# Empty places of a token list: a real token with weight zero, or a token number past the end

## The chip, the cores and the metric

The kernel runs on one core of one Trainium2 chip. The metric is the device time of one execution in microseconds (us); lower is better. In the profile PE is the matrix engine (PEld its weight loads), DVE the vector engine, ACT the scalar engine, POOL the general engine that also issues the indirect DMAs, and SP the engine that issues most plain DMAs.

## The reference

A block with two halves. The first is a gated recurrent layer over 4 sequences of 1024 tokens of width 256. The second is a mixture of experts: each token is given to the two best of eight experts, and the two results are weighted and added to the token. All arithmetic is float32.

```python
h = _layernorm(x) * (1 + ca) + sa
x = x + ga * attn(h)              # rms norm, four 256x512 products, sigmoid gates,
                                  # a scan over the tokens, a 512x256 product, + h
h = _layernorm(x) * (1 + cb) + sb
gate = softmax(h @ Wg + bg); topk_scores, topk_idx = top_k(gate, 2)
combine_w = normalised topk_scores, put at topk_idx
for e in range(8):
    y = _gelu(h @ W1[e] + b1[e]) @ W2[e] + b2[e]
    output = output + y * combine_w[..., e:e + 1]
x = x + gb * output
```

## The kernel before

**First half.** The 4096 tokens go through in eight chunks of 512 (`c_` from 0 to 7, two for each sequence `b`). The order of work on every engine is written out by hand. In a chunk, `project(c_, hc)` is called for four column groups (`hc` 0 to 3), and each issues four products on PE (L432). Between them stand the steps of neighbouring chunks: for the next chunk `a_square`, `a_root` (L387), `a_scale` (L391 to L394) and `a_turn` (transposes on PE, L406); for the chunk before it `o_pe` (L469), `o_resid`, `f_stats` (L216) and `f_norm`; for the one before that `f_turn` and `f_gate`. The square roots of `a_root` and of the two norms are done on POOL as a power (`L387`, `L216`), so the chain for the next chunk's transposes is: ACT squares, DVE L386, POOL L387, DVE L391 to L394, PE L406.

**Routing.** Once a sequence `b` is complete, `r_first`, `r_second`, `r_rank_pe` and `r_place` work out, for each token and each of its two experts, its place in that expert's list. The lists are one DRAM tensor `lists`: a region of 4096 places for each expert and one spare block of 256, and a place holds a pair (token number, weight). `pre`, built at the start by a memset, an iota and a bitwise_and (L188, L189, L266), fills all places first with (place mod 256, weight 0). `r_place` puts the writes of the real pairs into a waiting line, 16 scatters of 128 pairs for a sequence (8 columns for each of the two choices, "in"). For sequence 0 it puts 32 further scatters ahead of them (4 columns by 8 experts, "out"; L673 to L701): they write pairs of weight 0 into the first 256 places of an expert, counted back from the end, with tokens that did not choose this expert, so that a block whose list turns out short doesn't name one token twice. `drain(n)` takes `n` scatters off the line and issues each on POOL behind a tiny memset of `between` (L564, L568). It is called with 6 after each `project`. The first "in" scatter waits for all "out" scatters to have landed. A scatter's semaphore is one of eight used in turn, so from the ninth on each one waits for the landing of the eighth before it.

**Second half.** The lists are cut into blocks of 256 places, `j` from 0. The first 8 blocks use tokens of sequences 0 and 1 alone and start in the last chunk. For each block `fetch_rows` gathers its 256 rows of `hx` (normed token and gate, 2 KB each) into `hb` by two indirect DMAs of 128 rows (L836), `fetch_entries` loads the pairs into `ent` (L823), `fetch_weights` loads 2 MB of weights (L854, L856), `b_turn` transposes (L878), `b_up` and `b_down` multiply (L894, L912), and two indirect DMAs add the results into the rows of `out` (L926). `fetch(j)` issues the gathers of block `j + 2` and the weights of `j + 1`. A block that has at most 128 real places is computed as a half block (`_True` in the profile; its second half is gathered but not multiplied); from block 32 on each block stands inside a branch that asks whether it exists. An `ent` buffer is used again four blocks later, an `hb` buffer three blocks later.

Of the kernel before, what the change touches and what calls it, by code (L numbers as in the profile page):

```python
# [9 lines left out]
F32 = mybir.dt.float32  # L10
I32 = mybir.dt.int32
AF = mybir.ActivationFunctionType
ALU = mybir.AluOpType
# [6 lines left out]
def tile_adaln_block(  # L20
# [32 lines left out]
    nc = tc.nc  # L53
    P = 128
    B, S, D = x.shape
    H = W_out.shape[0]
    E, _, F = W1.shape
    T = B * S
# [8 lines left out]
    TK = 256  # L67
    HK = TK // P
    LN_EPS = 1e-5
    RMS_EPS = 1e-8  # L70
    TOPK_EPS = 1e-8
    FAR = float(1 << 20)
    NJ = (2 * T + E * (TK - 1)) // TK
    BPE = T // TK
    NE = 8
# [7 lines left out]
    lists = dram.tile([n_places, 2], I32, tag="lists", name="lists")  # L83
# [8 lines left out]
    small = ctx.enter_context(tc.tile_pool(name="small", bufs=2))  # L92
    xpool = ctx.enter_context(tc.tile_pool(name="blocks", bufs=2))
# [91 lines left out]

    n_pre = n_places // P
    pre = setup.tile([P, n_pre, 2], I32, tag="pre", name="pre")
    nc.gpsimd.memset(pre, 0)  # L188
    nc.gpsimd.iota(pre[:, :, 0], [[1, n_pre]], base=0, channel_multiplier=n_pre % TK)  # L189

    expo = const.tile([P, 2, TPB], F32, tag="expo", name="expo")
    nc.gpsimd.memset(expo[:, 0, :], -0.5)
# [70 lines left out]
    nc.scalar.dma_start(out=b1_sb, in_=b1.rearrange("e (c p) -> (e c) p", p=P))  # L263
    nc.scalar.dma_start(out=wg_sb, in_=Wg.rearrange("(k p) e -> p k e", p=P))
    nc.scalar.dma_start(out=bg_sb, in_=bg.rearrange("(o e) -> o e", o=1).broadcast_to((P, E)))
    nc.vector.tensor_single_scalar(pre[:, :, 0], pre[:, :, 0], TK - 1, ALU.bitwise_and)  # L266
    X[0]["stats"] = stats(X[0]["x"], "a0")
    shift(0)
    a_norm(0)
# [50 lines left out]
    def load_mda(b: int):  # L320
        if b < B:
            MDA[b] = deep.tile([P, 2, D], F32, tag="mda", name=f"mda_{b}")
            nc.sync.dma_start(out=MDA[b], in_=rows[b : b + 1, :2, :].broadcast_to((P, 2, D)))
# [209 lines left out]
    R = {}  # L533
# [17 lines left out]
            R[b]["p"][:, ts(i, TPB), :], pl, bg_sb.unsqueeze(1).broadcast_to((P, TPB, E))  # L551
        )

    scattered = {"out": [], "in": []}

    waiting = []
    between = const.tile([P, 1], F32, tag="between", name="between")

    def scatter(place, what, kind):
        waiting.append((place, what, kind))  # L560

    def drain(n: int):
        for _ in range(min(n, len(waiting))):
            nc.gpsimd.memset(between, 0.0)  # L564
            scatter_now(*waiting.pop(0))

    def scatter_now(place, what, kind):
        ins = nc.gpsimd.indirect_dma_start(  # L568
            out=lists[:, :],
            out_offset=IndirectOffsetOnAxis(ap=place, axis=0),  # L570
            in_=what,
            in_offset=None,
            bounds_check=E * T - 1,
            oob_is_err=False,
        )

        for other in scattered[kind]:
            tc.declare_no_dep(ins.ins, other.ins, reason="other places")
        if kind == "in" and not scattered[kind]:
            wait_for(ins, scattered["out"])  # L580
        scattered[kind].append(ins)

    def r_softmax(b):
        p = R[b]["p"]
# [82 lines left out]
    def r_place(b):  # L667
        pick, pay, key, pr = (R[b][n] for n in ("pick", "pay", "key", "pr"))
        rank = small.tile(sh, F32, tag="rank", name=f"rank_{b}", bufs=1)
        nc.vector.tensor_add(rank, pr[:, :NT, :], over(count))  # L670
        nc.vector.tensor_add(count, count, pr[:, NT, :])

        if b == 0:  # L673

            nm = 2 * HK
            shn = [P, nm, E]
            gap = small.tile(shn, F32, tag="gap", name="gap", bufs=1)
            at = small.tile(shn, F32, tag="at", name="at", bufs=1)  # L680
            no = small.tile(shn, F32, tag="no", name="no", bufs=1)
            ati = small.tile(shn, I32, tag="ati", name="ati", bufs=1)
            payn = small.tile([P, nm, 2], I32, tag="payn", name="payn", bufs=1)
            nc.gpsimd.memset(payn, 0)
            nc.vector.tensor_copy(payn[:, :, 0], token[:, :nm])

            nc.vector.tensor_sub(
                gap, token[:, :nm].unsqueeze(2).broadcast_to(tuple(shn)), rank[:, :nm, :]
            )
            nc.vector.scalar_tensor_tensor(  # L690
                at, gap, -1.0, head.unsqueeze(1).broadcast_to(tuple(shn)), ALU.mult, ALU.add
            )
            nc.vector.tensor_scalar(no, gap, float(TK), FAR, ALU.is_ge, ALU.mult)
            nc.vector.tensor_add(at, at, no)
            nc.vector.scalar_tensor_tensor(
                at, R[b]["chose"][:, :nm, :], FAR, at, ALU.mult, ALU.add
            )
            nc.vector.tensor_scalar_add(ati, at, float(TK - 1))
            for n in range(nm):
                for e in range(E):  # L700
                    scatter(ati[:, n, e : e + 1], payn[:, n, :], "out")  # L701

        nc.vector.tensor_add(rank, rank, over(head))
        for r in range(2):
            place = small.tile([P, NT], F32, tag=f"place{r}", name=f"place{r}_{b}")
            placei = small.tile([P, NT], I32, tag=f"placei{r}", name=f"placei{r}_{b}")
            nc.vector.tensor_mul(key, pick[r], rank)
            nc.vector.tensor_reduce(place, key, AX.X, ALU.add)
            nc.vector.tensor_copy(placei, place)
            for n in range(NT):  # L710
                scatter(placei[:, n : n + 1], pay[r][:, n, :], "in")


    def blocks_of(shift: float):
# [84 lines left out]
    def turns(pool, n: int, shape, dtype, tag: str, j: int):  # L799

        slots = kept.setdefault(tag, [None] * n)
        if slots[j % n] is None:
            slots[j % n] = pool.tile(shape, dtype, tag=f"{tag}{j % n}", name=f"{tag}_{j % n}", bufs=1)
        return slots[j % n]

    def seen(j: int):
        return EARLY_B * S if j < NE else T
# [57 lines left out]
    def wait_for(ins, others):  # L865
        for other in others:
            tc.add_manual_dep(
                ins.ins, other.ins.name,
                mybir.DependencyInfo(mybir.DependencyClass.Sync, mybir.DependencyReason.DATA),
                reason="all of it is there",  # L870
            )
# [35 lines left out]
    def b_down(j: int, half: bool = False, mid=None):  # L907
        g, w2, b2b, ent, hb = (BK[j][n] for n in ("g", "w2", "b2b", "ent", "hb"))
        for t in range(1 if half else HK):
            py = ps_y.tile([P, D], F32, tag="y", name=f"pye_{j}_{t}_{half}")  # L910
            for fc in range(FC):
                nc.tensor.matmul(  # L912
                    py,
                    lhsT=g[:, fc, ts(t, P)],
                    rhs=w2[:, fc, :],
                    start=(fc == 0),
                    stop=(fc == FC - 1),
                )
            yb = xpool.tile([P, D], F32, tag="yb", name=f"yb_{j}_{t}_{half}", bufs=4)
            nc.vector.tensor_add(yb, py, b2b)  # L920
            nc.vector.scalar_tensor_tensor(  # L921
                yb, yb, ent[:, t, 1:2].bitcast(F32), hb[t][:, D:], ALU.mult, ALU.mult
            )
            if t > 0:
                nc.gpsimd.memset(between, 0.0)
            ins = nc.gpsimd.indirect_dma_start(  # L926
                out=out_rows[: seen(j)],
                out_offset=IndirectOffsetOnAxis(ap=ent[:, t, 0:1], axis=0),
                in_=yb, in_offset=None, bounds_check=seen(j) - 1, oob_is_err=True,
                compute_op=ALU.add,  # L930
            )
            for other in BK[j]["acc"]:
                tc.declare_no_dep(ins.ins, other.ins, reason="a block's tokens are distinct")
            BK[j]["acc"].append(ins)
            if t == 0 and mid is not None:
                mid()
# [20 lines left out]
    for c_ in range(NCH):  # L957
# [40 lines left out]
        if not more:  # L998
            fetch_weights(0)
            for j in range(NE):  # L1000
                fetch_entries(j)

            wait_for(BK[0]["ld"], scattered["out"] + scattered["in"])
            fetch_rows(0)
            fetch_rows(1)
        if part == 0:
            if c_ == 0:
                setup_ctx.close()
                pools["w"] = ctx.enter_context(tc.tile_pool(name="weights", bufs=2))
            load_gb(b)  # L1010
            load_mda(b + 1)
            if c_ == 0:
                load_mdf(1)

# [85 lines left out]
    for j in range(3, sure_whole):  # L1100
        fetch(j)
        drain(5)
        if j + 2 == NE:
            wait_for(BK[NE]["ld"], scattered["in"])
            for ins in BK[NE]["gathers"]:
                wait_for(ins, hx_stores + hx_gates)
        work(j)
        if j == NE:
            for ins in BK[j]["acc"]:
                wait_for(ins, x1_stores)  # L1110
# [52 lines left out]
```

## Time and profile before

| | |
|---|---|
| time, median of 3 runs | 830.62 us (830.11 to 831.63) |
| the profiled execution's own time | 836.73 us |
| its span, first to last instruction | 835.0 us |
| PE busy | 806.2 us, 97% |
| POOL busy | 332.9 us, 40% |
| POOL, 32 "out" scatters (L568 `lists<-payn,ati`) | 32.8 us, mean 1024 ns |
| POOL, 64 "in" scatters (L568 `lists<-pay,placei`) | 66.0 us, mean 1031 ns |
| POOL, gathers of `hb` from `ent` (L836) | 60, mean 1058 ns |
| POOL, additions into `out` of whole blocks, `ent` (L926) | 46, mean 1602 ns |
| granted PE clock, mean | 0.988 |
| bytes moved by DMA | 136.53 MB |

An engine's busy time is a sum over instructions. A "wait" line names who ended an engine's idle time. The profiled execution took 6.1 us longer than the median of the unprofiled ones.

### The profile page before, as it was taken

Reading aid. Unit: us, or ns where it says so; the run is one execution under the profiler, and the core shown is the slowest. Engines: PE = TensorE matmul, PEld = TensorE weight load, DVE = VectorE, ACT = ScalarE, POOL = GpSimd, SP = SyncE. Lnnn points to the kernel's source line nnn. Section 1 sums busy time; section 2 is a strip of 40 time slices with the busy share of each in tenths; the row PEclk is TensorE's granted clock in tenths of the full one; section 3 lists DMA queues with packets and bytes.
Section 4 is the critical chain, followed back from the end, with each engine's and each line's share of the span. In section 5 each row is a group of like instructions: output and inputs, shape, how many; then the busy total and the mean of one; then the engine's idle time right before and its main releaser. Section 6 shows DMA issues by size and latency. Waiting matters only on the chain. (4 is left out here: it accounts for less than half of the span.)

```text
span 835.0 us, 10666 instructions
## 1 busy us (share of the span) xinstructions
PE 806.2 (97%) x3447; PEld 607.7 (73%) x3447; DVE 349.9 (42%) x814; ACT 250.9 (30%) x577; POOL 332.9 (40%) x438
## 2 busy tenths in 40 slices
PE   6999999999979999999999999999999999999983
PEld 2454656465636467888888888888888888888973
DVE  4787776798569757444111111111121212111211
ACT  4434343534343425131313122222222121312221
POOL 2001010116577843478844343424343333434432
PEclk9999999999989999999999999999999999999997
DMA  8041221118301356397878787777777777878795
GB/s 304 0 130 44 90 89 62 51 44 75 46 27 32 77 134 208 91 257 194 207 230 228 205 211 219 210 200 222 204 208 219 208 228 203 230 201 224 210 335 182
DMA packets 111217, 136.53 MB, mean 164 GB/s; under 512 B 25576, under 2 KB 94252, under 8 KB 111152
## 3 DMA queue, kind: packets, MB, share of 16 engines
q1 hardware_dynamic: 86624, 102.15, 42.1%
q0 software_dynamic: 18800, 28.81, 15.2%
q10 hardware_dynamic: 5728, 4.77, 2.5%
q8 instruction: 33, 0.54, 0.3%
q14 instruction: 32, 0.26, 0.1%
HBM read 113.92 MB, written 21.78 MB: 163 GB/s over the span
## 5 line engine op out<-in xcount | busy, mean ns | idle before, releaser
L912 PE MATMUL pye_False<-w,g_False 128*128 128x256 f32 x992 | 220.9, 381 | 1.1 <-DVE x L482 1.1
L894 PE MATMUL ph_False<-xT,w 128*128 128x256 f32 x992 | 219.2, 379 | 0.0
L894 PEld LDWEIGHTS ph_False<-xT,w 128*128 128x128 f32 x992 | 188.3, 190 | 25.5
L912 PEld LDWEIGHTS pye_False<-w,g_False 128*128 128x128 f32 x992 | 187.1, 191 | 25.6 <-issue 1.1
L903 ACT ACTIVATE g_False<-ph_False,bb 128x256 f32<-128x256 f32 x248 | 104.1, 471 | 313.1 <-issue 225.6
L926 POOL DMA_INDIRECT out_dram<-yb_False,ent x46 | 73.7, 1602 | 188.5 <-DVE yb_False L921 188.5
L880 DVE COPY xT<-ptx 128x512 f32<-128x512 f32 x37 | 25.5, 690 | 200.5 <-PE ptx L878 200.5
L920 DVE TENSOR_TENSOR yb_False<-pye_False,b2b 128x256 f32<-128x256 f32 x62 | 26.3, 424 | 155.0 <-PE pye_False L912 155.0
L836 POOL DMA_INDIRECT hb<-hx,ent x60 | 63.5, 1058 | 28.0 <-issue 16.1
L568 POOL DMA_INDIRECT lists<-pay,placei x64 | 66.0, 1031 | 15.7 <-issue 11.8
L432 PE MATMUL pu<-hT,wu_sb 128*128 128x512 f32 x128 | 61.9, 607 | 0.0
L432 PE MATMUL pk<-hT,wk_sb 128*128 128x512 f32 x128 | 61.0, 599 | 1.0 <-ACT hT L408 1.0
L432 PE MATMUL pgo<-hT,wu_sb 128*128 128x512 f32 x128 | 60.6, 596 | 0.0
L432 PE MATMUL pgi<-hT,wu_sb 128*128 128x512 f32 x128 | 60.1, 592 | 0.0
L469 PE MATMUL pya<-wo,z 128*128 128x256 f32 x256 | 56.6, 379 | 0.0
L469 PEld LDWEIGHTS pya<-wo,z 128*128 128x128 f32 x256 | 48.6, 190 | 9.5 <-issue 3.3
L216 POOL TENSOR_TENSOR rstd_f<-rstd_f,expo 128x4 f32<-128x4 f32 x8 | 8.2, 1026 | 101.3 <-DVE rstd_f L215 101.3
L432 PEld LDWEIGHTS pgo<-hT,wu_sb 128*128 128x128 f32 x128 | 24.7, 193 | 31.5 <-issue 27.6
L432 PEld LDWEIGHTS pgi<-hT,wu_sb 128*128 128x128 f32 x128 | 24.3, 190 | 30.6 <-issue 30.6
L432 PEld LDWEIGHTS pu<-hT,wu_sb 128*128 128x128 f32 x128 | 24.2, 195 | 27.4 <-issue 25.2
L432 PEld LDWEIGHTS pk<-hT,wk_sb 128*128 128x128 f32 x128 | 23.1, 190 | 25.1 <-issue 20.7
L568 POOL DMA_INDIRECT lists<-payn,ati x32 | 32.8, 1024 | 20.6 <-DMA lists<-payn,ati 13.1
(198 smaller groups left out, 781.1 us busy)
## 6 DMA issues: line engine op xcount, KB each, us to landing
w<-in_L_ffn_W_dram SPq DMA_DIRECT2D x74, 1024.0 KB, 6.5
b2b<-in_L_ffn_b_dram SPq DMA_DIRECT2D x37, 128.0 KB, 6.8
hx<-gb ACTq DMA_DIRECT2D x4, 1024.0 KB, 8.8
out_dram<-x SPq DMA_DIRECT2D x8, 512.0 KB, 4.0
hx<-h SPq DMA_DIRECT2D x8, 512.0 KB, 4.1
x<-in_L_attn_x_dram SPq DMA_DIRECT2D x7, 512.0 KB, 6.7
wu_sb<-in_L_attn_W_ugg_dram SPq DMA_DIRECT2D x3, 512.0 KB, 6.9
mdf<-rows SPq DMA_DIRECT2D x4, 384.0 KB, 8.1
```

Source lines behind the costliest of these rows:

```text
L216: nc.gpsimd.tensor_tensor(rstd, rstd, expo[:, 0, :], ALU.pow)
L432: nc.tensor.matmul(ps, lhsT=w[:, k, col : col + P], rhs=hT[:, k, :], start=(k == 0), stop=(k == KC - 1),)
L469: nc.tensor.matmul(py[:, t, :], lhsT=z[hc][:, ts(2 * q + t, P)], rhs=wo[:, hc, :], start=(hc == 0), stop=(hc == HC - 1),)
L568: ins = nc.gpsimd.indirect_dma_start(out=lists[:, :], out_offset=IndirectOffsetOnAxis(ap=place, axis=0), in_=what, in_offset=None, bounds_ ...
L836: nc.gpsimd.indirect_dma_start(out=g, out_offset=None, in_=hx[: seen(j), :], in_offset=IndirectOffsetOnAxis(ap=BK[j]["ent"][:, t, 0:1], ax ...
L880: nc.vector.tensor_copy(xT, pt)
L894: nc.tensor.matmul(ph[:, u, :], lhsT=w1[:, k, ts(fc, P)], rhs=xT[:, k, :n], start=(k == 0), stop=(k == KC - 1),)
L903: nc.scalar.activation(g[:, fc, :n], ph[:, u, :], AF.Gelu_apprx_tanh, bias=bb[:, fc : fc + 1])
L912: nc.tensor.matmul(py, lhsT=g[:, fc, ts(t, P)], rhs=w2[:, fc, :], start=(fc == 0), stop=(fc == FC - 1),)
L920: nc.vector.tensor_add(yb, py, b2b)
L926: ins = nc.gpsimd.indirect_dma_start(out=out_rows[: seen(j)], out_offset=IndirectOffsetOnAxis(ap=ent[:, t, 0:1], axis=0), in_=yb, in_offse ...
```

## The change

The list is filled with token number T (4096, one past the last) instead of place mod 256, so the iota and the bitwise_and go. The gathers leave such rows out and keep what the buffer held; the additions leave them out too (`oob_is_err` becomes False). In the early blocks the bound is 2048. As the rows left in `hb` must be numbers, all six `hb` buffers are cleared once, on POOL in chunk 1 ahead of that chunk's `a_root`. The 32 "out" scatters, their places and their wait are gone. In the text of the loop, `load_mdf(1)` of chunk 0 ends up below a condition that never holds, so that load is gone; the same rows are loaded again in chunk 1 as before.

```diff
-    nc.gpsimd.memset(pre, 0)
-    nc.gpsimd.iota(pre[:, :, 0], [[1, n_pre]], base=0, channel_multiplier=n_pre % TK)
+    nc.gpsimd.memset(pre, T)
...
-    nc.vector.tensor_single_scalar(pre[:, :, 0], pre[:, :, 0], TK - 1, ALU.bitwise_and)
...
-        if kind == "in" and not scattered[kind]:
-            wait_for(ins, scattered["out"])
...
-        if b == 0:
...
-            nc.gpsimd.memset(payn, 0)
...
-            for n in range(nm):
-                for e in range(E):
-                    scatter(ati[:, n, e : e + 1], payn[:, n, :], "out")
...
             for n in range(NT):
-                scatter(placei[:, n : n + 1], pay[r][:, n, :], "in")
+                waiting.append((placei[:, n : n + 1], pay[r][:, n, :]))
...
+    def clear_rows():
+
+        for j in range(3):
+            for t in range(HK):
+                nc.gpsimd.memset(turns(xpool, 3, [P, 2 * D], F32, f"hb{t}", j), 0.0)
...
-                in_=yb, in_offset=None, bounds_check=seen(j) - 1, oob_is_err=True,
+                in_=yb, in_offset=None, bounds_check=seen(j) - 1, oob_is_err=False,
                 compute_op=ALU.add,
...
         if part == 0:
             if c_ == 0:
...
             load_gb(b)
             load_mda(b + 1)
+        elif c_ == 1:
+            clear_rows()
             if c_ == 0:
                 load_mdf(1)
```

More of the change, by code (lines that the diff above doesn't have):

```diff
@@ L71, in tile_adaln_block @@
     TOPK_EPS = 1e-8
-    FAR = float(1 << 20)
     NJ = (2 * T + E * (TK - 1)) // TK
@@ L552, in f_gate @@
         )
-    scattered = {"out": [], "in": []}
+    scattered = []
     waiting = []
     between = const.tile([P, 1], F32, tag="between", name="between")
-    def scatter(place, what, kind):
-        waiting.append((place, what, kind))
     def drain(n: int):
@@ L564, in drain @@
             nc.gpsimd.memset(between, 0.0)
[L565 to L578, printed above, removed]
-        if kind == "in" and not scattered[kind]:
-            wait_for(ins, scattered["out"])
-        scattered[kind].append(ins)
+            place, what = waiting.pop(0)
+            ins = nc.gpsimd.indirect_dma_start(
+                out=lists[:, :],
+                out_offset=IndirectOffsetOnAxis(ap=place, axis=0),
+                in_=what,
+                in_offset=None,
+                bounds_check=E * T - 1,
+                oob_is_err=False,
+            )
+            for other in scattered:
+                tc.declare_no_dep(ins.ins, other.ins, reason="other places")
+            scattered.append(ins)
     def r_softmax(b):
@@ L671, in r_place @@
         nc.vector.tensor_add(count, count, pr[:, NT, :])
-        if b == 0:
[L677 to L683, printed above, removed]
-            nc.gpsimd.memset(payn, 0)
[L685 to L698, printed above, removed]
-            for n in range(nm):
-                for e in range(E):
-                    scatter(ati[:, n, e : e + 1], payn[:, n, :], "out")
         nc.vector.tensor_add(rank, rank, over(head))
@@ L1001, in tile_adaln_block @@
                 fetch_entries(j)
-            wait_for(BK[0]["ld"], scattered["out"] + scattered["in"])
+            wait_for(BK[0]["ld"], scattered)
             fetch_rows(0)
@@ L1103, in tile_adaln_block @@
         if j + 2 == NE:
-            wait_for(BK[NE]["ld"], scattered["in"])
+            wait_for(BK[NE]["ld"], scattered)
             for ins in BK[NE]["gathers"]:
```

## The prediction

> **What bounds the kernel now.** I read the page's busy times first, then the slices, then who waited, then the order of time around the one hole. (The chain that ended last has three pieces and tells nothing here.)
>
> ```profile
> PE 806.2 (97%) x3447; PEld 607.7 (73%) x3447; DVE 349.9 (42%) x814; ACT 250.9 (30%) x577; POOL 332.9 (40%) x438
> PE   6999999999979999999999999999999999999983
> POOL 2001010116577843478844343424343333434432
> PEclk9999999999989999999999999999999999999997
> ```
>
> PE is the bound nearly everywhere: only slices 1, 12 and the last two (20.9 us each) have holes. Freeing POOL or the DMAs is worth something only there. Slice 12 is also where POOL is fullest and the clock dips. PE's own waits name the cause:
>
> ```profile
> PE pta L406 <- DVE u L394: 4.6, 1, 4.6
> ```
>
> In order of time on PE (start, duration, then the idle time before it):
>
> ```profile
> 195.41 1.04 PE L406 MATMUL pta<-ident,u 128*128 128x128 f32 x8
> ...
> 238.05 2.05 PE L406 MATMUL pta<-ident,u 128*128 128x128 f32 x8 [4.56 <-DVE u L394]
> 239.89 3.62 PE L432 MATMUL pu<-hT,wu_sb 128*128 128x512 f32 x4
> 243.31 2.35 PE L432 MATMUL pgo<-hT,wu_sb 128*128 128x512 f32 x4
> 245.50 1.88 PE L432 MATMUL pk<-hT,wk_sb 128*128 128x512 f32 x4
> ```
>
> The transposes of chunk 6 come 4.56 us late, and the next products run at half speed: from the transposes to the next pk takes 7.45 us here (238.05 to 245.50) and 4.31 us a chunk earlier (195.41 to 199.72). The hole costs 4.56 + 3.14 = **7.7 us**. Who is late is on POOL:
>
> ```profile
> 211.46 1.60 POOL L568 DMA_INDIRECT lists<-payn,ati  x1 [7.58 <-DMA lists<-payn,ati]
> ...
> 222.50 0.97 POOL L568 DMA_INDIRECT lists<-payn,ati  x1 [5.50 <-DMA lists<-payn,ati]
> ...
> 227.32 1.06 POOL L216 TENSOR_TENSOR rstd_f<-rstd_f,expo 128x4 f32<-128x4 f32 x1
> ...
> 236.02 1.07 POOL L387 TENSOR_TENSOR ss<-ss,expo 128x4 f32<-128x4 f32 x1
> ```
>
> The power for a_root (L387) had its operand at 223.50 (DVE L386, 223.34 + 0.16), but stood behind 24 "out" scatters, two of which waited 7.58 and 5.50 us for earlier ones to land. It ran 12.5 us late; DVE L391 to L394 and PE follow.
>
> The other hole is the end. Half blocks follow each other every 7.46 us while nothing is late (787.02 to 794.48); the next three steps take 9.78, 9.45 and 8.70 us, 5.5 us too much. Block 35 (j from 0) is the last.
>
> ```profile
> 795.19 0.37 SPq L823 DMA_DIRECT2D ent<-lists  x1
> ...
> 801.60 1.05 POOL L836 DMA_INDIRECT hb<-hx,ent  x1 [4.09 <-PE pye_True L912]
> ...
> 809.62 0.55 PE L878 MATMUL ptx<-ident,hb 128*128 128x128 f32 x3 [1.17 <-DMA hb<-hx,ent]
> ```
>
> The add of block 31 (issued 788.51) lands, by the DMA view 5.3 to 7.4 us later, and only then does SP load the pairs of block 35 into the same buffer (795.19); those rows are gathered from 801.60 on, and PE waits for them at 809.62. The end thus hangs on landings: add, pairs, gather, and at last the final add (823.67).
>
> **What the Trainium skill says.** TensorE: Matmul & The Clock Gate, "Part 1: The HAM clock gate (the "warmup" mystery)": after an idle window of about 3.4 us the clock falls to half, and about 3.4 us of work bring it back. The trace agrees: after 4.56 us of idling the granted clock is 0.50 from 238 to 244 us. DMA: Bandwidth & Descriptors, "SWDGE vs HWDGE vs iDMA": for DMAs issued from GpSimd, indirect ones included, software there computes the descriptors. The trace shows about 1 us of POOL for each, and the same for scatters whose entries are nearly all left out (974 ns median of the 32 "out") as for full ones (979). I know of no price there for an entry that a bound leaves out.
>
> **The change part by part**, against the profiled execution's 836.73 us.
>
> 1. *32 "out" scatters gone.* 32.8 us busy, 33 memsets and 20.6 us of idling leave POOL. The 16 "in" scatters take their slots: 6 and 6 in chunk 4, 4 in chunk 5, instead of 24 ahead of L387. Suppose the same waits at the same places: the 14th is done at 216.9, the 15th waits to 222.50, the 16th ends at about 224.8. L216 then runs to 225.9 and L387 to 226.9, against 237.09. The transposes could start 10.2 us earlier, at 227.9; PE frees itself at 233.49. So the hole closes with 5.6 us to spare: **-7.7 us**. In chunk 6 L387 (276.45) stood behind scatters too, without a hole on PE (279.77); it now stands ahead of them.
> 2. *The wait of the first "in" scatter* (3.02 us at 251.69) goes; POOL only, no PE hole there: 0. POOL at 277 to 299 also loses its backlog, so the last pairs for the early blocks land sooner, and PE did not wait for block 0's rows at 317.68: 0. Everything there moves with PE; SP still has w and b2b ahead of the pairs (302.09 against 304.04), so at most 2 us of earliness is to be had, nothing that PE waits for.
> 3. *Seven small DVE operations of r_place* (187.12 to 188.36, and 0.84 us of waiting) go; DVE had u of chunk 5 ready at 191.4 and PE transposed it at 195.41: 0.
> 4. *Six memsets of hb* in chunk 1. Nearest row: L188, 128x516 int32, 0.53 us, so 3.2 us. They follow L216 (ends 67.89) and end near 71.1; L387 comes at 73.02. Cover: DVE's project work. Without it (memsets at twice the price) L387 is 1.3 us late, and u is ready at 76.9 for transposes at 81.01: 0.
> 5. *Front:* the iota (0.36 us) and bitwise_and (0.29) go. PE's first product also needs sc, ready at 4.01 (DVE); bn_stats may start 0.2 us sooner if x has landed. The first projections begin at 20.34 behind that chain: 0 to -0.2, taken -0.1.
> 6. *load_mdf(1) of chunk 0:* one SP issue of 0.42 us (46.61) and 384 KB; the x load behind it lands long before its use: 0.
> 7. *Entries left out.* 36 blocks are computed (31 whole, 5 half), 38 gathered: 9728 rows for 8192 real pairs, so 1536 rows of 2 KB, 3.1 MB of 136.5, are not moved, and 384 of 8576 additions. Whole blocks hide it (PE without idle from 366 to 788). At the end each half block loses at least 256 KB (its second half) of some 2.8 MB (2 MB weights, 128 KB b2b, 512 KB rows, 128 KB additions), while the DMAs are 81% busy: 9% of the load. That entries left out move no bytes is seen on two quiet stretches with seven scatters each, nearly all out of range in the first and all real in the second:
>
> ```profile
> q0 software_dynamic: 224, 0.00, 1.5%
> ...
> q0 software_dynamic: 224, 0.01, 1.8%
> ```
>
>    Against it, they land no sooner: 7.6, 8.6, 7.5 and 5.3 us for out-of-range scatters from 237 to 243, where full ones took 4.6, 5.1, 5.9 and 6.3 from 251 to 258, a mean of 7.25 against 5.5. Bounds: the lost 5.5 us and about 1 us of the final landing come back (-6.5), or the three hops through leave-outs (add, gather, final add) are 1.8 us later each (+5.4). I take -0.7: less load and slow landing nearly cancel, in favour of less load because 252 GB/s are flowing there.
> 8. *Additions with leave-out.* Not shown before. Upward bound 0.6 us more for each, downward the 1031 ns of a leave-out scatter, 0.57 less. Two of them lie on the end's path: -1.1 to +1.2, taken 0. Elsewhere POOL is at 38%.
>
> Sum in the profiled execution: -7.7 - 0.1 - 0.7 = -8.5, to 828.2. It is 6.1 us above the median of the runs. PE's stream cannot be quicker without a profile, so those 6.1 lie in waits: front 6.0, this hole 7.7, one at 340 us 2.6, tail 5.5, after the last PE work 12.6, outside the span 1.7, in all 36.1. Spread evenly, the hole is 7.7 x (1 - 6.1/36.1) = 6.4 us in the runs. I take 6.4 + 0.1 + 0.7 = 7.2: 830.6 - 7.2 = **823.4 us**.
>
> **The rivals.**
> - *The hole is mostly the profile's.* If the landings that POOL waited for are quicker unprofiled (13.1 us of waits in two places, and 6.1 us to explain), the power is in time by itself once they are 5 us shorter, and only items 5 and 7 remain: 829.5. For it: the difference of 6.1. Against: full scatters would still keep POOL busy. 13%.
> - *Leave-outs are slow, and it ends slower.* At the end, where each landing decides the next step, three hops. At the quiet stretch's +1.8 us each, +5.4 leaves 825 to 826; to be slower than before they must lose 6.5 us, over 2.2 each, and at double the quiet price (3.6) it is +10.8 - 6.5 = 835. For it: the scatter landings above. Against: the second half of every half block then moves nothing. 7%, part of it within 0.2%.
> - *A longer jam in chunk 4.* Full scatters meet the 1 MB store of gb at 192.3 (it took 15.3 us to land). The waits must grow by over 5.6 us to reopen a hole. In chunk 6 full scatters met the same store and landed within 7.8 us. Price: each us beyond, up to the old hole: 830. 4%.
> - *The tail gains its bound:* 830.6 - 6.4 - 6 = 818.2. 6%.
> - *Leave-outs are moved after all:* then only item 7 goes, 824.1; inside the likeliest case.
>
> **How the numbers follow.** The likeliest, 70%: 823.4, its own range 820.5 to 826.5 (hole of 4.5 to 7.7, tail +1.8 to -2). The range 818.5 to 829.3 takes in most of the strong tail and of the small hole. About 0.2%, 1.7 us, is what a measurement can tell from no change. Faster: 70 + 6 + 7 of the first rival + 3 of the others, 86%; within: 8; slower: 6.
>
> **What would show it.** In the profile after: no wait of pta on u near 233 us, clock 1.0 there; L387 of that chunk right behind its operand; no payn; PE's first transposes of half blocks without waits for hb; q0 with about 25.5 MB instead of 28.81. Wrong if that hole is there, if steps of half blocks grow beyond 9.8 us, or if additions take over 2.2 us on POOL.

## The result, and the profile after

| | before | after |
|---|---|---|
| median, six runs each | 830.94 us (830.11 to 832.16) | 826.44 us (824.72 to 828.35) |
| the profiled execution | 836.73 us | 828.35 us |
| its span | 835.0 us | 826.6 us |
| granted PE clock, mean | 0.988 | 0.992 |

The changed kernel is faster: the ratio is 0.9948, 95% interval 0.9931 to 0.9964, or 4.5 us. Ratios, and the gains given with them, are worked out from all executions but those over 1.5% above the fastest of their kernel, and not from the medians, so the two can differ by up to 0.2%. The forecast was 823.4 us, 7.2 us less than before. From profile to profile the difference is 8.4 us, where the forecast's sum had 8.5.

The page of the kernel after, engines and slices (20.7 us each), and its row of the software DMA queue:

```profile
PE 802.2 (97%) x3447; PEld 606.4 (73%) x3447; DVE 348.9 (42%) x806; ACT 250.7 (30%) x577; POOL 300.4 (36%) x378
...
PE   6999999999999999999999999999999999999992
...
POOL 2003010108203730778743433434342433334432
PEclk9999999999999999999999999999999999999997
...
q0 software_dynamic: 17776, 25.25, 13.7%
...
L891 POOL DMA_INDIRECT out_dram<-yb_False,ent x46 | 73.8, 1604 | 188.7 <-DVE yb_False L886 188.7
```

The dip of PE and of its clock in slice 12 is gone, POOL has 60 instructions and 32.5 us less, the software queue moves 25.25 MB instead of 28.81, and an addition of a whole block takes 1604 ns of POOL on average where it took 1602.

The place of the hole, in order of time on PE in the kernel after (start, duration):

```profile
232.67 1.04 PE L403 MATMUL pta<-ident,u 128*128 128x128 f32 x8
233.54 1.88 PE L429 MATMUL pu<-hT,wu_sb 128*128 128x512 f32 x4
235.26 1.88 PE L429 MATMUL pgo<-hT,wu_sb 128*128 128x512 f32 x4
236.98 1.88 PE L429 MATMUL pk<-hT,wk_sb 128*128 128x512 f32 x4
```

The transposes have no idle time before them, and `pk` follows 4.31 us after their start, the undisturbed distance. On POOL, in order of time, the memsets of `hb`, the power of their chunk, the last "in" scatter and the power ahead of the old hole:

```profile
67.19 2.85 POOL L769 MEMSET hb<- 128x512 f32 x6
72.36 1.01 POOL L384 TENSOR_TENSOR ss<-ss,expo 128x4 f32<-128x4 f32 x1 [2.32 <-DVE nmr L221]
...
210.31 0.97 POOL L559 DMA_INDIRECT lists<-pay,placei  x1 [0.19 <-issue]
...
222.99 1.01 POOL L384 TENSOR_TENSOR ss<-ss,expo 128x4 f32<-128x4 f32 x1 [6.04 <-DVE nmr L221]
```

The last of the 16 "in" scatters is issued at 210.31. The power for `a_root` (now L384) of chunk 6 comes at 222.99 after 6.04 us of free POOL, instead of 236.02 behind 24 scatters. The six memsets of `hb` end at 70.04, and the power of that chunk still follows at 72.36 after 2.32 us of free time.

At the end, PE's half blocks in the kernel after:

```profile
794.27 3.73 PE L859 MATMUL ph_True<-xT,w 128*128 128x128 f32 x32
798.79 0.30 PE L843 MATMUL ptx<-ident,hb 128*128 128x128 f32 x1 [0.79 <-DMA hb<-hx,ent]
799.34 0.55 PE L843 MATMUL ptx<-ident,hb 128*128 128x128 f32 x3 [0.25 <-DMA hb<-hx,ent]
...
803.50 3.81 PE L859 MATMUL ph_True<-xT,w 128*128 128x128 f32 x32 [0.17 <-DMA w<-in_L_ffn_W_dram]
...
807.91 3.62 PE L877 MATMUL pye_True<-w,g_True 128*128 128x256 f32 x16
```

The half blocks start at 771.24, 778.70, 786.16, 794.27 and 803.50: steps of 7.46, 7.46, 8.11 and 9.23 us, where before had 7.46, 7.46, 9.78 and 9.45. From the first start to the last `pye_True` it is 36.67 us instead of 39.21.

Five marks give the balance between the two profiles, earlier by: `pk` after the hole 8.5 us (245.50 to 236.98; 7.7 of it the hole, nearly all of the rest already there before it), first half block 8.3 (779.55 to 771.24), last `pye_True` 10.9 (818.76 to 807.91), last addition 9.5 (823.67 to 814.13), end of the span 8.4. So the last half blocks added 2.5 to the hole's gain, and 2.4 us were **lost again** between the last product and the end. The forecast had no such loss.

Two questions follow. Why is the gain of the runs 4.5 us when the profiles show 8.4? And which part of the edit gave what: the scatters that are gone, or the entries that are left out?

### The profile page after: what moved, and what is told of

It reads as the page before. It is cut to its first block, busy times and chain, and to the rows that moved or that the text cites. A ratio compares the mean times of both kernels' runs of the same rounds, so it can differ in the third digit from the quotient of the medians.

```text
span 826.6 us, 10561 instructions
## 1 busy us (share of the span) xinstructions
PE 802.2 (97%) x3447; PEld 606.4 (73%) x3447; DVE 348.9 (42%) x806; ACT 250.7 (30%) x577; POOL 300.4 (36%) x378
## 3 DMA queue, kind: packets, MB, share of 16 engines
q0 software_dynamic: 17776, 25.25, 13.7%
## 5 line engine op out<-in xcount | busy, mean ns | idle before, releaser
L891 POOL DMA_INDIRECT out_dram<-yb_False,ent x46 | 73.8, 1604 | 188.7 <-DVE yb_False L886 188.7
L559 POOL DMA_INDIRECT lists<-pay,placei x64 | 68.2, 1066 | 12.6 <-issue 11.5
L429 PE MATMUL pu<-hT,wu_sb 128*128 128x512 f32 x128 | 60.2, 592 | 0.0
L446 DVE TENSOR_TENSOR nu<-nu,pu 128x512 f32<-128x512 f32 x32 | 22.0, 686 | 45.4 <-PE pu L429 33.8
```

What stands on the lines that cost most here:

```text
L429: nc.tensor.matmul(ps, lhsT=w[:, k, col : col + P], rhs=hT[:, k, :], start=(k == 0), stop=(k == KC - 1),)
L446: nc.vector.tensor_mul(nu, nu, product(wu_sb, hc * P, "u"))
L559: ins = nc.gpsimd.indirect_dma_start(out=lists[:, :], out_offset=IndirectOffsetOnAxis(ap=place, axis=0), in_=what, in_offset=None, bounds_ ...
L891: ins = nc.gpsimd.indirect_dma_start(out=out_rows[: seen(j)], out_offset=IndirectOffsetOnAxis(ap=ent[:, t, 0:1], axis=0), in_=yb, in_offse ...
```

## The experiments

They were run in three groups of four, each on one chip and beside the kernel before on that chip. In all of them the differences are small against the spread of the kernel before, so intervals matter.

**First group: one part of the change at a time** (before on this chip: median 833.41 us, 828.27 to 837.73, 41 runs).

*The kernel before, unchanged, once more.*

> The kernel before, unchanged, for a second profile and a spread of spans and granted clocks. Theory 1 (the hole near 234 us is in every execution, and the prediction overrated something else): PE waits for the transposes of chunk 6 by 4 to 5 us again, clock 0.988 in all runs, all runs near 830.9. Theory 2 (the hole varies, and the first profile had an uncommonly long one): the wait in this profile is under 3 us or absent, the clock of the runs lies above 0.988, and the two landings that POOL waits for take less than 13.1 us in sum.

834.60 us (829.68 to 838.80, 14 runs), ratio 1.0012 (0.9987 to 1.0037). Its profiled execution took 836.56 us. Among PE's waits in it:

```profile
PE pta L406 <- DVE u L394: 4.5, 1, 4.5
```

The hole is there again, 7.1 us by the forecast's reckoning (idle time, plus what the distance from `pta` to `pk` exceeds 4.31). But 836.6 us lies inside the spread of its own unprofiled runs, which goes from 829.7 to 838.8 (in the first comparison it ended at 832.2). The kernel before thus varies by several us from execution to execution, and the 6.1 us by which the first profiled execution lay above its median need be no price of the profile. The other profiled executions speak against such a price: the eleven that have further runs of the same kernel beside them lie from 2.1 us below to 3.3 us above the median of those runs.

*The scatters gone, the rest as before.* The block that makes the 32 "out" scatters is cut from before. Short lists may then name a token twice in a gather, which changes no amount of work.

```diff
-        if b == 0:
...
-            for n in range(nm):
-                for e in range(E):
-                    scatter(ati[:, n, e : e + 1], payn[:, n, :], "out")
```

> The kernel before with only the 32 out scatters (and their seven DVE operations and two waits) taken away; the fill, the gathers, the additions and the start stay as before, and empty places keep real tokens with weight 0, so a short list could name a token twice. Theory 1: -6 to -8 us against before, and the changed kernel is then not faster than this one (its leave-outs lose 2 to 3 us at the end). Theory 2: -3 to -4 us, with the rest of the changed kernel's -4.5 coming from the start and the end.

830.24 us (828.19 to 834.28, 22 runs), ratio 0.9959 (0.9946 to 0.9971): 3.4 us faster. No wait of `pta` is left. The end is no quicker than before; in order of time on PE:

```profile
799.30 5.31 PE L864 MATMUL ph_True<-xT,w 128*128 128x128 f32 x32 [2.83 <-DMA w<-in_L_ffn_W_dram]
```

The fourth half block waits 2.83 us for its weights and then runs partly at a lower clock (5.31 us for 3.73).

*The entries left out, the scatters kept.* The kernel after, with the "out" scatters, their order and the wait put back. What is left of the change is the new start (fill, memsets of `hb`, one load less) and the entries that gathers and additions leave out, called leave-outs below:

```diff
+        if b == 0:
...
+            nc.gpsimd.memset(payn, T)
...
+            for n in range(nm):
+                for e in range(E):
+                    waiting.append((ati[:, n, e : e + 1], payn[:, n, :], outs))
```

> The changed kernel with the 32 out scatters put back ahead of the in scatters, with their places, lanes and wait as before; they write the pair of an empty place, so the result is unchanged. What is left of the change is the fill, the memsets of hb, the leave-outs at the end. Theory 1: the hole returns in full, 6 to 8 us slower than the changed kernel, so 832 to 834. Theory 2: it returns in part, 3 to 4 us, so about 829.5 to 830.5, with 1 us or less against before.

829.78 us (827.39 to 831.94, 12 runs), ratio 0.9948 (0.9930 to 0.9966): about 4 us faster than before **although the hole is there**. Its waits, of PE and of POOL:

```profile
PE pta L403 <- DVE u L391: 5.2, 1, 5.2
...
POOL lists L561 <- DMA lists<-payn,ati: 18.9, 5, 7.6
```

So the leave-outs and the new start are worth several us by themselves, where the forecast gave them 0.7 and 0.1.

*The scatters kept, but all out of range.* As the last one, with every place of the "out" scatters moved past the bound:

```diff
-            nc.vector.tensor_scalar_add(ati, at, float(TK - 1))
+            nc.vector.tensor_scalar_add(ati, at, float(TK - 1) + FAR)
```

> As the run with the out scatters put back, but all 32 have every place out of range: POOL issues them all, and nothing is written. If POOL's issue time alone makes the hole (24 scatters at 1.28 us ahead of the power for a_root), the hole stays as in that run. If it is the landings of the written ones that POOL waits for, 24 x 1.28 = 31 us from 187 on end near 220, L387 is in time, there is no hole and the time is that of the changed kernel, 826.4.

825.30 us (823.21 to 827.52, 6 runs), ratio 0.9897 (0.9866 to 0.9927). POOL issues as many scatters as in the kernel before, and `pta` waits for nothing. In the stretch from 186 to 230 us these scatters land after a median of 2.2 us:

```profile
lists<-payn,ati POOLq DMA_INDIRECT x27, 2.2
```

POOL's waits for them in the whole execution:

```profile
POOL lists L561 <- DMA lists<-payn,ati: 2.8, 1, 2.8
```

That is 2.8 us in place of 18.9. So it is not POOL's time for the issues that makes the hole, it is the landing of those entries that really are written. This also refutes a reading of the forecast, which took leave-out scatters to land later (7.25 us against 5.5): with all entries left out they land sooner than full ones. The two kernels have the same instructions, so the pairs that are written cost 4.5 us in the runs (829.78 against 825.30; by the two intervals, uncertain by about 3 us). Of all kernels here this one has the lowest ratio to before, the kernel after included, though it never ran beside that one; the section on the prediction has a likely part of the reason.

**Second group: what jams, and does order matter** (before on this chip: median 837.90 us, 832.46 to 851.47, 15 runs).

*The kernel after again.*

> The changed kernel once more, beside before on one chip, to set the four earlier runs against it. If the parts add (scatters gone -3.2, rest of the change -3.6 on the chip of the first four), it is at -6.5 to -8 against before and equals the run with all out places out of range (-8.1). If the start and the leave-outs bring nothing without the scatters, it is at -3 to -4.

829.79 us (827.73 to 832.98, 7 runs), ratio 0.9917 (0.9883 to 0.9952): 7.0 us, close to the forecast's 7.2, on a chip where before is longer and varies more; the interval reaches from 4 to 10 us.

*The scatters kept out of the way of the power.* Before, with chunk 5's first two `drain(6)` emptied and its last two doubled:

```diff
-        drain(6)
+        drain(0 if c_ == 5 else 6)
...
-        drain(6)
+        drain(12 if c_ == 5 else 6)
```

> The kernel before with all its scatters, but in chunk 5 the first two drains of six are issued with the third and fourth (twelve each), so that a_root's power L387 stands ahead of them. Nothing else changes. Theory A (the hole costs its full 7 us in every execution): no wait of pta on u, and -6 to -8 against before. Theory B (in usual executions it costs 3 to 4): -3 to -4. Theory C (the gain of the scatters' removal is not the hole but their traffic): no gain although the wait on u is gone.

845.86 us (9 runs), ratio 1.0088 (1.0043 to 1.0133): **slower**, a miss of what was on record, where every theory had a gain or none. POOL and PE in order of time:

```profile
280.54 1.06 POOL L387 TENSOR_TENSOR ss<-ss,expo 128x4 f32<-128x4 f32 x1
...
282.56 2.05 PE L406 MATMUL pta<-ident,u 128*128 128x128 f32 x8 [11.21 <-DVE u L394]
```

The transposes of chunk 6 are in time (232.61, no idle time ahead of them), but the hole moved to the next chunk's transposes and grew to 11.21 us of idling. The backlog on POOL was only pushed back, and was paid at the next place where PE needed POOL. As an undoing it tells only that the hole follows the scatters, which the other runs show more cleanly.

*The same scatters into a tensor of their own, places 8 bytes apart, and then 128 bytes apart.* Both are the kernel after with the "out" scatters put back, but written into a tensor `side` that nobody reads, so that neither the lists nor their order are touched. One profiled execution each.

```diff
+            into, most = (side, E * T * 16) if kind is outs else (lists, E * T)
...
-            nc.vector.tensor_scalar_add(ati, at, float(TK - 1))
+            nc.vector.tensor_scalar(ati, at, float(TK - 1), 16.0, ALU.add, ALU.mult)
```

(The near one has 1 in place of 16.)

> The changed kernel with the 32 out scatters, written into a tensor of their own at the same spacing of 8 bytes. If the jam of the DMAs from 192 to 224 comes from many 8-byte writes close together, it is here too: gb and hx stores land after 15 us or more, and POOL waits for landings. If it came from writing into the lists among other pairs, it is gone.

> As the run before, with the places 128 bytes apart instead of 8. If neighbouring writes of several DMA engines to one stretch of memory make the jam, the stores land in 3 to 6 us, POOL waits for no landing and there is no hole. If the mere number of 8-byte writes makes it, everything is as with 8 bytes of spacing.

Near, from the waits of POOL and PE:

```profile
POOL side L563 <- DMA side<-payn,ati: 15.4, 4, 7.9
...
PE pta L404 <- DVE u L392: 7.3, 1, 7.3
```

The share of the DMA engines that is busy from 186 to 230 us (40 slices of 1.1 us, in tenths), near and then far:

```profile
DMA  0000049998938996310000000099693098289321
```

```profile
DMA  0000009960067000000000000069520000000000
```

Far, POOL and PE in order of time:

```profile
225.25 1.06 POOL L385 TENSOR_TENSOR ss<-ss,expo 128x4 f32<-128x4 f32 x1
...
232.70 1.04 PE L404 MATMUL pta<-ident,u 128*128 128x128 f32 x8
```

Near, the jam (transfers that crawl while POOL waits for landings) and the hole stand as in before (hole 9.9 us), though another tensor is written. Far, the DMA engines are free after each burst, POOL waits for no landing, and PE has no idle time ahead of the transposes. The two kernels differ in the distance between the 8-byte places. The number of writes and their size are the same. What jams in the near one is thus **many short writes next to each other**: where they run, the stores of `gb` and `h` crawl too. By the same view's row of rates, near falls from 346 GB/s to between 21 and 62 for the next five slices, while far holds 350, 378 and 209 and is through. Times of one execution (838.57 and 837.82 us) decide nothing here: the far one has 7.4 us of issue gaps in `pye_False` elsewhere, whose cause is open.

**Third group: do the parts add up, and one more edit** (before on this chip: median 832.48 us, 829.34 to 837.62, 32 runs).

*The kernel after a third time; the scatters alone gone; the leave-outs alone.* The same three kernels as above, on one chip together.

> The changed kernel, as one corner of a square on one chip: before, scatters gone, out scatters kept, changed. If the two parts are independent, its gain over before is the sum of the gains of the next two runs within 2 us. From the two chips so far -5 to -8 us.

> Before without the 32 out scatters, second chip. If the hole is worth its 7 us of the profile in usual executions, -6 to -8 against before; if it was worth what the first chip said, -2.4 to -4.5.

> The changed kernel with the out scatters put back, second chip: all that start, clearing and leave-outs bring by themselves. The prediction's items 4 to 8 say -0.8; the first chip said -2.8 to -5.8. Leave-outs land late (my slower rival): 0 or slower than before. Leave-outs take load off the end: -2 to -5, with the steps of the half blocks closer to 7.46 us than in the runs without leave-outs.

| | median, us | ratio to before | gain by the ratio, us |
|---|---|---|---|
| scatters gone | 830.28 (12 runs) | 0.9959 (0.9943 to 0.9976) | 3.4 |
| leave-outs | 830.69 (21 runs) | 0.9968 (0.9953 to 0.9984) | 2.7 |
| both, the kernel after | 827.30 (6 runs) | 0.9921 (0.9895 to 0.9946) | 6.6 |

The parts add within the intervals: 0.41% and 0.32% make 0.73%, against 0.79% for both. And the hole itself varies. The profiled execution with the leave-outs alone shows on PE:

```profile
235.13 1.49 PE L403 MATMUL pta<-ident,u 128*128 128x128 f32 x8 [1.99 <-DVE u L391]
...
276.52 1.49 PE L403 MATMUL pta<-ident,u 128*128 128x128 f32 x8 [1.34 <-DVE u L391]
```

That is 2.5 us in the old place and 1.9 in the next chunk, clock included, for the same scatters that cost 7.7, 7.1 and 7.6 us at the old place in three other executions. Even so PE is late by nearly as much afterwards: it starts the first early block at 338.53, against 332.04 in the profiled execution of the kernel after on this chip, 6.5 us later.

*One more edit.* In the kernel after, PE waits 1.08 us at 331.71 for `x` (`o_resid`), ahead of the first early block, because DVE has `f_gate`'s work first. `o_resid(last)` is put ahead of `f_gate(last - 1)`:

```diff
-    f_gate(last - 1)
     o_resid(last)
+    f_gate(last - 1)
```

> The changed kernel with one more edit: at the start of the second half DVE adds the residual of the last chunk (o_resid) before it takes the gate scores of the chunk before it (f_gate), so that the output buffers of the first down product come free about 1 us sooner. If the 1.08 us wait of pye on that addition, and the half-speed clock that follows it in some executions (8.83 us against 7.07 to 7.14), are worth what the trace shows: -1 to -2.8 against the changed kernel. If DVE's order there hides nothing: the same time.

826.08 us (825.49 to 826.54, 6 runs), ratio 0.9907 (0.9884 to 0.9931), 1.2 us below the kernel after beside it, with intervals that overlap, so a gain is not shown by the times. The trace shows what the edit does. The kernel after, then this version:

```profile
331.71 8.83 PE L877 MATMUL pye_False<-w,g_False 128*128 128x256 f32 x32 [1.08 <-DVE x L479]
```

```profile
329.11 1.85 PE L540 MATMUL pl<-wg_sb,hT 128*128 128x8 f32 x16
330.81 7.15 PE L877 MATMUL pye_False<-w,g_False 128*128 128x256 f32 x32
```

The wait is gone and the block runs at its full pace: 1.08 + 1.68 = 2.8 us on PE at this place between these two executions. Only the 1.08 us are surely the edit's, as the block also ran at full pace in some executions that have the wait (last section).

## Why the prediction was right, and where not

**The jam and the hole (items 1 and 2): mechanism right, but part of the gain did not reach the end.** In the trace every step came as told: the power right behind its operand (222.99), the transposes on time, no half-speed products, and the hole's 7.7 us gone between two marks on PE. The 16 "in" scatters were done at 211.3, not at 224.8, as no landing held them up. But removing the scatters alone was worth 3.4 us on two chips, where item 1 had 6.4. How much earlier five marks come in the profiled executions shows where the rest went (us; means of two executions of before and of each single part, and of three of the kernel after; the first mark is the first `pye_False`):

| change | first early block | first half block | last `pye_True` | last addition | end |
|---|---|---|---|---|---|
| scatters go, without leave-outs | 8.7 | 8.8 | 6.7 | 6.3 | 4.8 |
| scatters go, with leave-outs | 7.0 | 6.1 | 6.7 | 6.4 | 3.6 |
| leave-outs come in, with scatters | 1.8 | 2.3 | 4.2 | 4.1 | 5.4 |
| leave-outs come in, without scatters | 0.0 | -0.4 | 4.2 | 4.1 | 4.1 |

Without the scatters PE is 6 to 9 us earlier at the second half, as item 1 said. Two things lie between that and the 3.4 us of the runs.

- *The scaling to the runs.* The forecast took the 6.1 us between profile and median for a price of profiling that lies in PE's waits, and spread it over them. No such price shows (see the repeat of before). How long the hole is in a median run stays open: the written pairs cost 4.5 us in the runs and 7.1 in their two profiled executions (spans of 829.5 and 822.4). So 6.4 came from a reason that does not hold, and no run refutes its size.
- *The end got longer.* From the start of the last addition to the end of the span:

| kernels | with "out" scatters in the program | without |
|---|---|---|
| no leave-outs | 11.33, 10.94, 10.67 | 12.55, 12.72 |
| leave-outs | 9.84, 9.86, 9.78, 10.34, 10.78 | 12.47, 12.78, 12.71, 12.82 |

(One number for each profiled execution, in us; the last two on the left are those with the tensor of their own.) Whether the scatters are in the program changes the last stretch by 1.7 us in the mean (without leave-outs) to 2.6 us (with them). The landing of the last addition is not the reason. The kernel after, then the one with all places out of range (us from issue to landing at the end of the line):

```profile
out_dram<-yb_True,ent POOLq DMA_INDIRECT x1, 3.8
```

```profile
out_dram<-yb_True,ent POOLq DMA_INDIRECT x1, 3.7
```

From that landing to the end of the span it is 8.7 us in the first and 6.1 in the second. In the eight profiled executions that show this landing it is 6.0 to 6.1 us in the four with the scatters and 8.7 to 8.8 in the four without. As the out-of-range scatters write nothing, it is not what they write; what else of them makes it is open. The forecast left this stretch as it was. Given back 2.7 us, the 3.4 would be about 6, near item 1's 6.4; this is an estimate, which takes the ends of the profiled executions for those of the runs.

**The leave-outs (item 7): the term that was too small.** Taken at 0.7 us, they are worth, with the new start, 2.7 us on one chip and about 4 on another. From the first half block to the last `pye_True`, nine profiled executions with leave-outs take 35.6 to 38.0 us, mean 36.6; five without take 38.3 to 43.1, median 38.6. The forecast let less load and slow landing nearly cancel. Slow landing was a misreading: the 7.25 us were those of scatters issued while the ones ahead of them were still landing (those from 227 to 237 us took a median of 8.5 us). In the run with all places out of range, where no scatter ahead writes, they land after 2.2 us. Nor could "nearly all out of range" be read from "0.00 MB", a rounded figure, as seven scatters of 128 pairs are 7 KB in all. What the gain comes from is not shown. Near the end, from 770 us on, gathers land after a median of 5.6 to 6.0 us with leave-outs and 5.9 to 6.4 without; additions after 6.2 to 7.7 and 6.4 to 7.4, no sooner. Less load is argued only. The rival "leave-outs are slow" is refuted by the times, and the gain lies inside the bounds of -6.5 to +5.4. One of the forecast's signs did not come: two waits for `hb` are left at 798.79 and 799.34, 1.0 us in all.

**The two errors cancel.** What the scatters' going brought was 3.0 us less than forecast, what the leave-outs brought 2 to 3 us more: the forecast of 7.2 us stands against 4.5, 7.0 and 6.6 in three comparisons. The sum was right in part by luck, and the profile against profile (8.4 against 8.5) flatters it most: there the hole was the full 7.7, the half blocks gave 2.5, and the end took 2.4 back. That the profiles differ by 8.4 us and the runs by 4.5 is mainly the long profiled execution of before, 5.8 us above its median, where that of the kernel after lies 1.9 above.

**The items at zero** held. DVE's small operations and `load_mdf(1)` (items 3 and 6) leave no mark on PE. The memsets (item 4) took 2.85 us against 3.2 and were covered, with 2.32 us to spare. The front (item 5) shows nothing: the first projections start at 19.88 us instead of 20.34, but the repeat of before has 19.83. The additions (item 8) are unchanged at 1604 ns. The longer jam in chunk 4 did not come.

**On the Trainium skill.** DMA: Bandwidth & Descriptors, "Specifications", puts the shortest transfer at line rate at 512 bytes and says that shorter ones are read, modified and written back. The direction agrees with these runs: scatters of 8 bytes cost far more than their bytes. The page says nothing on the distance between them, and here the distance decided: at 8 bytes apart POOL waits 15.4 us for landings, at 128 bytes apart not at all. Why it does, no run here shows.

## What to carry to other kernels

Of a stall in one profiled execution, take its place and mechanism, but size it from several executions of the same kernel, and follow the gain to the last instruction: here it was whole in the middle and smaller at the end. A stream of tiny writes to adjacent places held up POOL and the transfers beside it; writing nothing, or writing 128 bytes apart, ended that, and issuing the stream later only moved the stall to the next step on the same engine. Leave-outs cost the issuing engine as much as before. Scatters that leave everything out landed much sooner; for gathers and additions with some leave-outs the end of the kernel became shorter, and why is open.

## What the runs showed of the hardware that was not expected

- *A short wait can cost the clock.* After the 1.08 us wait at 331.71 PE's granted clock was 0.60 from 331.7 to 336 us, and the block's products took 8.83 us instead of 7.15. TensorE: Matmul & The Clock Gate, "Part 1: The HAM clock gate (the "warmup" mystery)", speaks of idle windows of about 3.4 us; here 1.08 us of idling, behind 1.85 us of products with only 8 columns, was followed by a slow block in nine profiled executions (8.5 to 8.8 us) and not in four others (7.1 us) with the same wait. One of the four is of the kernel after itself (compare 331.71 above):

```profile
332.38 7.14 PE L877 MATMUL pye_False<-w,g_False 128*128 128x256 f32 x32 [1.08 <-DVE x L479]
```

- *Indirect scatters of out-of-range places* take 0.97 us of POOL each and land in 2.2 us, against some 6 us for full ones in the same stretch of the kernel after.
- *The last stretch of a program,* after its last DMA is issued, took 9.8 to 12.8 us; from the landing of that DMA it was 6.0 to 6.1 us with 32 scatters in the program 500 us earlier, whether they write or not, and 8.7 to 8.8 without them. The cause is open.
